# Cross attention on one core: the last transpose of a softmax put off, ring weights asked for ahead, a split sum, and a new order of the last outputs

## The chip, the core and the metric

The kernel runs on one NeuronCore of a Trainium2 chip. The time is the device time of one execution in microseconds; the figure before the change is the median of three runs. A core has five engines with a queue of instructions each: TensorE (PE, matmuls; PEld is its weight load), VectorE (DVE), ScalarE (ACT), GpSimd (POOL) and SyncE (SP), which in this kernel issues nearly all DMAs. Each queue runs in order, and engines wait for each other with semaphores. Lines such as L525 are lines of the kernel's source before the change.

## The reference, cut to what matters

`x` is 8 batches of 256 rows of 1024 values, `ctx` 8 batches of 256 rows of 1024. There are 32 heads of 32 columns. All is float32.

```
xn   = (x - mean) * rsqrt(var + 1e-5) * gamma + beta      # per row
Q    = heads(xn @ Wq.T);  K = V = heads(ctx)
p    = softmax(where(mask, Q K^T / sqrt(32), -inf))
out  = x + merge_heads(p V) @ Wout.T
```

## The kernel before, in words

**Slots.** The main loop (L870) runs over 64 slots `n`: batch `n // 8`, group of four heads `n % 8`. It is a software pipeline over groups. In slot `n` PE gets the scores of group `n + 1` (`scores`, L471), some steps of the output projection of the batch before (`product_steps`, L681), the product of the probabilities and values of group `n - 2` (`values`, L611), and a part of the queries of later batches (`make_q`, L332, or `query_product`, L432). The other engines get the softmax of group `n + 1` in the same slot. The order on each queue is the order in which the Python code emits instructions; nothing reorders it. Below, `i` is the place of a slot in its batch, `n % 8`.

**Softmax** (`softmax_parts`, L483). For each of four heads `j`, `exps(j)` masks and takes a row minimum on DVE (L506) and the exponential with its sum on ACT (L510). `normalize(j)` is a reciprocal on DVE (L517) and two scalings on POOL (L519). `blocks(j)` transposes 32 by 32 blocks on DVE into `pT` (L525), and `aside` copies half of the result on ACT into `pc` (L531), for two heads at a time. Four DMAs on SP then exchange partitions: `pT<-pT` (L591) and `pT<-pc` (L595), two of each. The last part, `tail`, holds `blocks(3)`, `aside(1)`, the four moves and, between the pairs of moves, the loads listed in `between`. `values(n)` needs it two slots later. `pT` and `pc` have three buffers each.

**A tail can be put off.** In the first batch and in softmaxes 57 to 62 it isn't emitted at once but put into `tails`, and the next softmax emits it after its own `exps(0)`. All others emit it at once (L597).

**Loads.** `between` holds, by slot, the keys (`load_k`, even slots), the values (`load_v`, odd slots), inputs of later batches, the residual rows for the outputs (`load_res`, L150, in slots `i` = 0 to 3), and `rings[n]`: weights for the queries that are kept in DRAM and brought into one SBUF tile, `ring`, three times in a batch from batch 3 on (`load_ring`, L399). T1 comes in slots `i` = 7 and 0, B11 in slot 2, T3 in slot 4, each as two transfers of 512 KB. They are used by `query_product` in slots `i` = 2, 4 and 6, and a new set can be brought in only after PE has read the old one.

**Query and output products** use a scheme of seven products of half-size blocks, with sums of blocks on POOL: `sum_x` (L422) for the inputs, `sum_at` (L664) for the attention results. A batch's seven output products accumulate in one PSUM bank; on its way DVE takes the state of the bank three times into the residual tiles (`store`, L723, and `take`, L719), and PE waits for that before it goes on in the bank. POOL has added the first product's part to three of the four residual tiles before (`add_p1`, L714). In the seventh batch's products (emitted in the last eight slots) the order differs (`ENDS`), and the sum S2 for them is emitted in slot 57.

**The end.** For the eighth batch the output projection is direct: `project` (L731) multiplies by the weights in eight chunks of 128 rows, for four outputs (`ends`: two row halves by two column halves of 512). A chunk `c` needs the attention result of head group `c`. The first output, `last`, is begun in slots 59 to 63. Then come `values(62)`, `values(63)` with their copies to SBUF (`copy_at`, L624), and the rest of the chunks, each output followed by `store`: an add on DVE and a store to DRAM. A matmul in float32 runs as two passes on PE.

Of the kernel before, what the change touches and what calls it, by code (L numbers as in the profile page):

```python
# [46 lines left out]
F32 = mybir.dt.float32  # L47
U8 = mybir.dt.uint8
AF = mybir.ActivationFunctionType
ALU = mybir.AluOpType  # L50

P = 128
# [7 lines left out]
def xattn_kernel(  # L60
# [11 lines left out]
    nc = tc.nc  # L72
    B, S, D = x.shape
# [3 lines left out]
    NQ = NC  # L77
# [9 lines left out]
    N = B * NQ  # L87
# [20 lines left out]
    NK = D // P // 2  # L108
# [14 lines left out]
    xs, ks, vs, rs = {}, {}, {}, {}  # L123
# [352 lines left out]
    def softmax(*args):  # L476
        for _ in softmax_parts(*args):
            pass
# [1 line left out]
    tails = []  # L480


    def softmax_parts(n, copies=(), between=(), hooks={}, fill=()):  # L483

        fill = list(fill)

        def fill_in():  # L490
            if fill:
                fill.pop(0)()

        pss = scs[n]
        pT = pTs[n] = ptp.tile([P, 2, NI, NH, NS, K], F32, tag="pT", name=f"pT_{n}")
        pc = asp.tile([P, NI, NH, NS, K], F32, tag="pc", name=f"pc_{n}")
        es, mns, dens = {}, {}, {}

        def exps(j, part=range(NS)):
            if 0 in part:  # L500
                es[j] = ep.tile([P, NS, T], F32, tag="e", name=f"e_{n}_{j}")
                mns[j] = sm.tile([P, NS], F32, tag="mn", name=f"mn_{n}_{j}")
                dens[j] = sm.tile([P, NS], F32, tag="den", name=f"den_{n}_{j}")
            e, mn, den = es[j], mns[j], dens[j]
            for s in part:
                nc.vector.tensor_tensor_reduce(  # L506
                    out=e[:, s, :], in0=pss[j][:, s, :], in1=mbs[n // NQ], scale=1.0,
                    scalar=NO_SCORE, op0=ALU.add, op1=ALU.min, accum_out=mn[:, s : s + 1],
                )
                nc.scalar.activation(  # L510
                    e[:, s, :], e[:, s, :], AF.Exp, bias=mn[:, s : s + 1], scale=-1.0,
                    accum_out=den[:, s : s + 1],
                )

        def normalize(j):
            rden = sm.tile([P, NS], F32, tag="rden", name=f"rden_{n}_{j}")
            nc.vector.reciprocal(rden, dens[j])  # L517
            for s in range(NS):
                nc.gpsimd.tensor_scalar(  # L519
                    es[j][:, s, :], es[j][:, s, :], rden[:, s : s + 1], 1.0,  # L520
                    ALU.mult, ALU.mult,
                )

        def blocks(j):
            nc.vector.transpose(  # L525
                pT[:, :, :, j, :, :].rearrange("p a i s k -> p (a i) s k"),
                es[j].rearrange("p s (b t) -> p b s t", t=K),
            )

        def aside(j):  # L530
            nc.scalar.copy(pc[:, :, ts(j, 2)], pT[:, 1, :, ts(j, 2)])  # L531

        if n == 0:
            for j in range(NH - 1):
                exps(j, (0,))
            yield
            exps(NH - 1, (0,))
            fill_in()
            yield
            for j in range(NH):  # L540
                exps(j, (1,))
            normalize(0)
            fill_in()
        else:
            exps(0)
            while tails:
                tails.pop()()
            late = "p1" in hooks
            if not late:
                for done in list(pvs):  # L550
                    copy_at(done)
            exps(1)
            for hook in hooks.get("soon", ()):
                hook()
            exps(2)
            normalize(0)
            for hook in hooks.get("p1", ()):
                hook()
            exps(3)
            if late:  # L560
                for done in list(pvs):
                    copy_at(done)
        if n <= NQ:
            for copy in copies:
                copy()
        for hook in hooks.get(0, ()):
            hook()
        normalize(1)
        fill_in()
        blocks(0)  # L570
        for hook in hooks.get(1, ()):
            hook()
        normalize(2)
        fill_in()
        blocks(1)
        aside(0)
        normalize(3)
        fill_in()
        blocks(2)
        while fill:  # L580
            fill_in()
        if n > NQ:
            for copy in copies:
                copy()

        def tail():
            blocks(3)
            aside(1)

            for r in range(2):  # L590
                nc.sync.dma_start(pT[ts(2 * r, K), 1], pT[ts(2 * r + 1, K), 0])  # L591
            for load in between:
                load()
            for r in range(2):
                nc.sync.dma_start(pT[ts(2 * r + 1, K), 0], pc[ts(2 * r, K)])  # L595

        if n < NQ or N - NQ < n < N - 1:  # L597
            tails.append(tail)
        else:
            tail()  # L600
        yield
# [16 lines left out]
    def copy_at(n):  # L618
        b, c = divmod(n, NQ)
        k, c = divmod(c, NK)  # L620
        if c == 0:
            ats[b, k] = atp.tile([P, NK, NS, NA, K], F32, tag="at", name=f"at_{b}_{k}")
        for r, pv in enumerate(pvs.pop(n)):
            nc.scalar.copy(  # L624
                ats[b, k][:, c, :, ts(r, 2), :], pv.rearrange("p a s k -> p s a k")
            )
# [22 lines left out]
    def operand(b, name):  # L649

        if name in ("S2", "S1"):
            return s2s[b]
        s, k = {"A11": (0, 0), "A12": (0, 1), "A21": (1, 0), "A22": (1, 1),
                "S3": (1, 0), "S4": (0, 1)}[name]
        return ats[b, k][:, :, s].rearrange("p c a k -> p c (a k)")

    def sum_at(b, name):
        if name == "S2":
            s2s[b] = up.tile([P, NK, P], F32, tag="s2", name=f"s2_{b}")
        one, two, op = {  # L660
            "S3": ("A11", "A21", ALU.subtract), "S2": ("A22", "S3", ALU.subtract),
            "S1": ("S2", "A11", ALU.add), "S4": ("A12", "S2", ALU.subtract),
        }[name]
        nc.gpsimd.tensor_tensor(operand(b, name), operand(b, one), operand(b, two), op)  # L664

    s2s, p1s = {}, {}

# [55 lines left out]
        nc.vector.tensor_tensor(r, pos[b] if po is None else po, r, ALU.add)  # L723
        nc.sync.dma_start(out[b, ts(s, P), ts(h, 512)], r)

    def project(po, b, s, h, chunks):

        for c in chunks:
            k, i = divmod(c, NK)
            w = {(0, 0): wo[:, B11], (1, 0): wo[:, B21], (1, 1): wo[:, B22], (0, 1): b12}[k, h]  # L730
            nc.tensor.matmul(  # L731
                po, ats[b, k][:, i, s].rearrange("p a k -> p (a k)"), w[:, i],
                start=(c == 0), stop=(c == NC - 1),
            )

# [94 lines left out]
    scores(0, (0,))  # L830
    for c in range(NC):
        copy_x0(1, c, nc.scalar if c < NC // 2 else nc.vector)
    first = softmax_parts(0, (partial(copy_q, 1),), (), {}, [
        partial(ln_stats, 1, 0), partial(ln_stats, 1, 1),
        partial(ln_norm, 1, 0, nc.vector), partial(ln_norm, 1, 1, nc.scalar),
    ])
# [33 lines left out]
    for n in range(N):  # L870
# [4 lines left out]
            between.append(partial(load_v, n + 1))  # L875
        elif n % 2 == 0 and n + 4 < N:
            between.append(partial(load_k, n + 4))
        between += rings[n]
        if b >= 0:
            if b == B - 2 and i - 1 in (2, 5, 6):  # L880
                between.append(partial(send, b, *ENDS_TO[i - 1]))
# [39 lines left out]
            fill = [partial(ln_stats, *args, parts=(i,)) for args in stats[n] for i in range(3)]  # L921
            fill += [partial(blocks_x, *args) for args in trans[n]]
        if n + 1 < N:
            softmax(n + 1, copies, between, hooks, fill)
        else:
            copy_at(n - 2)
            for load in between:
                load()
        if b >= 0 and i == 1:
            sum_at(b, "S2")  # L930
        if n >= NQ:
            for args in stats[n]:
                ln_stats(*args)
# [12 lines left out]
        if b >= 0:  # L946
            for name in {0: ("S3",), 2: ("S4",), 3 if b == B - 2 else 5: ("S1",)}.get(i, ()):
                sum_at(b, name)
        for slot, name in ((n + 2, "S1"), (n + 1, "S2"), (n + 1, "S4"), (n - 1, "S3")):
            if slot in firsts:  # L950
                sum_x(firsts[slot], name)
# [10 lines left out]
            nc.gpsimd.tensor_scalar(gs, gam, NEG_SCALE, 1.0, ALU.mult, ALU.mult)  # L962
        if n < NQ:
            fold(n)
        if not new_qs[n] and n - 2 > N - NQ:

            chunks = [c for c in range(NQ) if N - NQ + c <= n - 3]
            if last is None:
                last = ps_q.tile([P, 512], F32, tag="pq", name="po_last")
                made = 0  # L970
            project(last, B - 1, 0, 0, chunks[made:])
            made = len(chunks)
# [3 lines left out]
    ends = [(B - 1, s, h) for h in range(NO) for s in range(NS)]  # L976
    pos = {end: ps_s.tile([P, 512], F32, tag="sc", name=f"po_{end[1]}_{end[2]}") for end in ends[1:]}
    pos[ends[0]] = last
    values(N - 2)
    copy_at(N - 2)  # L980
    again = xp.tile([P, NS, D], F32, tag="x", name="x_again")
    for s in range(NS):
        nc.sync.dma_start(again[:, s, :], x[B - 1, ts(s, P), :])
    for b, s, h in ends:
        rs[b, s, h] = again[:, s, ts(h, 512)]
    project(last, *ends[0], range(made, NQ - 2))
    project(pos[ends[1]], *ends[1], range(NQ - 2))
    values(N - 1)
    copy_at(N - 1)
    project(pos[ends[2]], *ends[2], range(NQ - 1))  # L990
    for i, end in enumerate(ends):
        project(pos[end], *end, range((NQ - 2, NQ - 2, NQ - 1, 0)[i], NQ))
        store(*end, pos[end])


# [38 lines left out]
```

## Time and profile before

| what | us |
|---|---|
| runs | 585.6, 586.97, 590.12 (median 586.97) |
| the profiled execution, its own time | 585.12 |
| its span, first to last instruction | 583.3 |
| PE busy | 570.0 (98%) |
| PE weight loads busy | 392.6 (67%) |
| DVE busy | 453.4 (78%) |
| ACT busy | 412.2 (71%) |
| POOL busy | 393.0 (67%) |
| DMA | 119.02 MB, 204 GB/s on average |

The granted PE clock is full throughout. The time between two starts of the scores is a slot's length: some 6 to 10 us. Ends of matmuls are modelled in the profile, so that a busy PE can hide short waits. A number in brackets after an instruction is the idle time of its engine just before it, and what ended that.

### The profile page before, as it was taken

To read this page: it belongs to the slowest core of one execution; us is meant where nothing else is said; L and a number is where in the kernel's file an instruction comes from. 1 tells how busy PE (TensorE), PEld (TensorE's weight loads), DVE (VectorE), ACT (ScalarE), POOL (GpSimd) and SP (SyncE) were. 2 spreads that over 40 slices of the span, in tenths; PEclk is the share of its full clock that TensorE was granted. 3 is DMA by queue.
4 is the path that set the end of the run, shared out by engine and by line. 5 is a ranking of instruction groups with operands and counts; after the bars stand their busy time and mean duration, and the time that the engine had idled before them with its cause. 6 is when DMAs were issued, how large, how long until landed. Compare 5 with 4: busy or idle time off the path is not lost.

```text
span 583.3 us, 19985 instructions
## 1 busy us (share of the span) xinstructions
PE 570.0 (98%) x7160; PEld 392.6 (67%) x7160; DVE 453.4 (78%) x1685; ACT 412.2 (71%) x1425; POOL 393.0 (67%) x662
## 2 busy tenths in 40 slices
PE   8999999999999999999999999999999999999997
PEld 7787785766657767667766776676776776645443
DVE  5878887888778888788886898688976787689701
ACT  4788887777668867687775976769775876679800
POOL 1568898899789886677448765587636864559700
PEclk9999999999999999999999999999999999999999
DMA  8557789756786778766887668857757776448551
GB/s 310 218 159 223 219 242 234 218 180 166 221 261 202 213 223 240 221 191 164 255 233 213 187 188 247 239 172 228 207 157 237 223 193 186 127 135 238 159 160 72
DMA packets 47907, 119.02 MB, mean 204 GB/s; under 512 B 9152, under 2 KB 9664, under 8 KB 47808
## 3 DMA queue, kind: packets, MB, share of 16 engines
q1 hardware_dynamic: 47520, 117.74, 68.6%
q8 instruction: 57, 0.93, 0.7%
q14 instruction: 42, 0.34, 0.2%
q10 hardware_dynamic: 288, 0.01, 0.0%
HBM read 66.33 MB, written 11.53 MB: 133 GB/s over the span
## 4 chain that ended last, share of the span: by engine, by line
PE 60%; POOL 14%; DVE 10%; DMA 7%; issue 4%; ACT 2%; SPq 2%; POOLq 0%; DVEq 0%; ACTq 0%
PE po_S L681 14%; PE pq_A L432 10%; POOL e L519 10%; PE pq L332 8%; PE sc L471 7%; PE pv L611 7%; PE po_A L681 6%; DVE e L506 4%; PE po L731 4%; DVE pT L525 3%; PE pq_S L432 2%; DMA wq<-in_wq_dram 2%; POOL sx L422 2%; DMA x<-in_x_dram 1%; DMA pT<-pT 1%
## 5 line engine op out<-in xcount | busy, mean ns | idle before, releaser
L519 POOL TENSOR_SCALAR e<-e,rden 128x256 f32<-128x256 f32 x512 | 235.7, 478 | 95.6 <-DVE rden L517 93.2
L510 ACT ACTIVATE e<-e,mn 128x256 f32<-128x256 f32 x512 | 253.9, 500 | 38.6 <-DVE mn L506 38.5
L525 DVE STREAM_TRANSPOSE pT<-e 128x512 f32<-128x512 f32 x256 | 181.2, 708 | 63.5 <-POOL e L519 52.5
L506 DVE CUSTOM_DVE_ANT_0 e<-sc,mb 128x256 f32<-128x256 f32 x512 | 185.5, 415 | 19.4 <-PE sc L471 19.1
L531 ACT COPY pc<-pT 128x512 f32<-128x512 f32 x128 | 79.0, 617 | 85.8 <-DVE pT L525 43.3
L510 ACT ACTIVATION_READ_ACCUMULATOR e<-e,mn 128x1 f32 x512 | 97.7, 191 | 0.0
L332 PE MATMUL pq<-xnT,wq 128*128 128x256 f32 (+1 forms) x368 | 84.1, 382 | 1.3 <-ACT qa L339 1.2
L332 PEld LDWEIGHTS pq<-xnT,wq 128*128 128x128 f32 x368 | 68.7, 190 | 15.8 <-issue 3.8
L611 PE MATMUL pv<-pT,v 64*32 64x128 f32 x4096 | 74.7, 274 | 1.9 <-ACT at L624 1.0
L611 PEld LDWEIGHTS pv<-pT,v 64*32 64x32 f32 x4096 | 57.3, 105 | 27.3 <-issue 12.8
L471 PEld LDWEIGHTS sc<-k,qa 32*128 32x128 f32 x1024 | 46.7, 184 | 42.9 <-issue 23.7
L681 PE MATMUL po_S<-wo,at 128*128 128x512 f32 x152 | 74.6, 608 | 0.9 <-DVE r L719 0.9
L471 PE MATMUL sc<-k,qa 32*128 32x256 f32 x1024 | 74.6, 401 | 0.1
L681 PE MATMUL po_A<-wo,at 128*128 128x512 f32 x128 | 60.6, 608 | 0.4 <-ACT qa L341 0.4
L681 PE MATMUL po_S<-wo,s 128*128 128x512 f32 x104 | 50.2, 607 | 0.5 <-DVE r L723 0.5
L517 DVE RECIPROCAL rden<-den 128x2 f32<-128x2 f32 x256 | 37.7, 147 | 7.5 <-ACT e L510 6.1
L506 DVE DVE_READ_ACCUMULATOR2_ANT mn<- 128x1 f32 x512 | 42.5, 83 | 0.0
L432 PEld LDWEIGHTS pq_A<-xnT,wq 128*128 128x128 f32 x320 | 37.3, 192 | 4.8 <-issue 3.8
L681 PEld LDWEIGHTS po_S<-wo,at 128*128 128x128 f32 x152 | 25.8, 190 | 21.2 <-issue 19.3
L681 PEld LDWEIGHTS po_A<-wo,at 128*128 128x128 f32 x128 | 22.6, 189 | 25.4 <-issue 21.4
L432 PE MATMUL pq_A<-xnT,wq 128*128 128x128 f32 x320 | 37.3, 275 | 0.0
L714 POOL TENSOR_TENSOR r<-r,p 128x512 f32<-128x512 f32 x18 | 23.1, 1284 | 14.1 <-DMA r<-in_x_dram 14.1
(82 smaller groups left out, 591.6 us busy)
## 6 DMA issues: line engine op xcount, KB each, us to landing
v<-in_kv_dram SPq DMA_DIRECT2D x32, 512.0 KB, 4.1
pT<-pT SPq DMA_DIRECT2D x128, 128.0 KB, 2.5
pT<-pc SPq DMA_DIRECT2D x128, 128.0 KB, 5.1
ring<-kept_T SPq DMA_DIRECT2D x18, 512.0 KB, 6.0
k<-in_kv_dram SPq DMA_DIRECT2D x32, 256.0 KB, 3.0
x<-in_x_dram SPq DMA_DIRECT2D x14, 512.0 KB, 5.1
r<-in_x_dram SPq DMA_DIRECT2D x28, 256.0 KB, 4.4
out_dram<-r SPq DMA_DIRECT2D x28, 256.0 KB, 3.8
```

The lines of the kernel that those rows point to most:

```text
L332: nc.tensor.matmul(pqs[n], wq[:, o, c, :], xnTs[b](c), start=(c == 0), stop=(c == NC - 1),)
L432: nc.tensor.matmul(pqs[b][:, o, :], w[:, c], x_[:, c], start=begins and o + c == 0, stop=c == NK - 1, skip_group_check=True,)
L471: nc.tensor.matmul(scs[n][j][:, s, :], qa[r, n % NQ, ts(s, P)], ks[n - n % 2][r, n % 2, :], start=True, stop=True,)
L506: nc.vector.tensor_tensor_reduce(out=e[:, s, :], in0=pss[j][:, s, :], in1=mbs[n // NQ], scale=1.0, scalar=NO_SCORE, op0=ALU.add, op1=ALU.m ...
L510: nc.scalar.activation(e[:, s, :], e[:, s, :], AF.Exp, bias=mn[:, s : s + 1], scale=-1.0, accum_out=den[:, s : s + 1],)
L517: nc.vector.reciprocal(rden, dens[j])
L519: nc.gpsimd.tensor_scalar(es[j][:, s, :], es[j][:, s, :], rden[:, s : s + 1], 1.0, ALU.mult, ALU.mult,)
L525: nc.vector.transpose(pT[:, :, :, j, :, :].rearrange("p a i s k -> p (a i) s k"), es[j].rearrange("p s (b t) -> p b s t", t=K),)
L531: nc.scalar.copy(pc[:, :, ts(j, 2)], pT[:, 1, :, ts(j, 2)])
L611: nc.tensor.matmul(pvs[n][r][j * HD : (j + 1) * HD], vs[n - n % 2][ts(r, 2 * K), i, ds(n % 2 * P + j * HD, HD)], pT[ts(r, 2 * K), :, i, j, ...
L681: nc.tensor.matmul(po, operand(b, name)[:, c], wo[:, which, c], start=begins and c == 0, stop=c == NK - 1, skip_group_check=not begins,)
L731: nc.tensor.matmul(po, ats[b, k][:, i, s].rearrange("p a k -> p (a k)"), w[:, i], start=(c == 0), stop=(c == NC - 1),)
```

## The change

There are five edits.

1. `DEFERRED = range(1, 5)`: the tails of softmaxes with `n % 8` from 1 to 4 are put off, in all batches.
2. `rings[n]` leaves `between` and becomes `ahead`, emitted just before the place where the tail is either emitted or put off.
3. S2 of the seventh batch is emitted in two parts: chunks 0 to 2 at the end of slot 56, after S3, and chunk 3 in slot 57.
4. The chunks of the last projections are put in another order around `values(62)` and `values(63)`. The first output is begun in slots 59 to 62 and no longer in slot 63.
5. The last of the four outputs is made in two column parts, 384 and 128 wide, each with its own matmuls, add and store; the second uses a PSUM tile of the `ps_v` pool.

```diff
+    DEFERRED = range(1, 5)
+
+    def softmax_parts(n, copies=(), ahead=(), between=(), hooks={}, fill=()):
...
-        if n < NQ or N - NQ < n < N - 1:
+        for load in ahead:
+            load()
+        if n < NQ or n % NQ in DEFERRED or N - NQ < n < N - 1:
             tails.append(tail)
         else:
             tail()
...
-    def sum_at(b, name):
-        if name == "S2":
+    def sum_at(b, name, c=slice(0, NK)):
+        if name == "S2" and c.start == 0:
...
-        nc.gpsimd.tensor_tensor(operand(b, name), operand(b, one), operand(b, two), op)
+        nc.gpsimd.tensor_tensor(
+            operand(b, name)[:, c], operand(b, one)[:, c], operand(b, two)[:, c], op
+        )
...
-    def project(po, b, s, h, chunks):
+    def project(po, b, s, h, chunks, cols=slice(0, 512)):
...
-                po, ats[b, k][:, i, s].rearrange("p a k -> p (a k)"), w[:, i],
+                po, ats[b, k][:, i, s].rearrange("p a k -> p (a k)"), w[:, i, cols],
...
-        between += rings[n]
...
-            softmax(n + 1, copies, between, hooks, fill)
+            softmax(n + 1, copies, rings[n], between, hooks, fill)
...
-            sum_at(b, "S2")
+            sum_at(b, "S2", *((slice(NK - 1, NK),) if b == B - 2 else ()))
...
+            if i == 0 and b == B - 2:
+                sum_at(b, "S2", slice(0, NK - 1))
...
-        if not new_qs[n] and n - 2 > N - NQ:
+        if not new_qs[n] and N - NQ + 2 < n < N - 1:
...
-    values(N - 2)
-    copy_at(N - 2)
...
-    project(last, *ends[0], range(made, NQ - 2))
-    project(pos[ends[1]], *ends[1], range(NQ - 2))
+    project(pos[ends[1]], *ends[1], range(NK))
+    project(last, *ends[0], range(made, NQ - 3))
+    values(N - 2)
+    copy_at(N - 2)
+    project(pos[ends[1]], *ends[1], range(NK, NQ - 3))
+    project(pos[ends[2]], *ends[2], range(NK))
+    project(last, *ends[0], (NQ - 3,))
+    project(pos[ends[1]], *ends[1], (NQ - 3,))
     values(N - 1)
     copy_at(N - 1)
-    project(pos[ends[2]], *ends[2], range(NQ - 1))
-    for i, end in enumerate(ends):
-        project(pos[end], *end, range((NQ - 2, NQ - 2, NQ - 1, 0)[i], NQ))
+    project(pos[ends[2]], *ends[2], range(NK, NQ - 1))
+    for i, end in enumerate(ends[:3]):
+        project(pos[end], *end, range((NQ - 2, NQ - 2, NQ - 1)[i], NQ))
         store(*end, pos[end])
+
+    b, s, h = ends[3]
+    r = rs.pop(ends[3])
+    for cols in (slice(0, 384), slice(384, 512)):
+        po = pos[ends[3]] if cols.start == 0 else ps_v.tile([P, P], F32, tag="pv", name="po_end")
+        po = po[:, : cols.stop - cols.start]
+        project(po, *ends[3], range(NQ), cols)
+        nc.vector.tensor_tensor(r[:, cols], po, r[:, cols], ALU.add)
+        nc.sync.dma_start(out[b, ts(s, P), ds(512 * h + cols.start, cols.stop - cols.start)], r[:, cols])
```

More of the change, by code (lines that the diff above doesn't have):

```diff
@@ L480, in xattn_kernel @@
     tails = []
-    def softmax_parts(n, copies=(), between=(), hooks={}, fill=()):
+    DEFERRED = range(1, 5)
+    def softmax_parts(n, copies=(), ahead=(), between=(), hooks={}, fill=()):
         fill = list(fill)
@@ L832, in xattn_kernel @@
         copy_x0(1, c, nc.scalar if c < NC // 2 else nc.vector)
-    first = softmax_parts(0, (partial(copy_q, 1),), (), {}, [
+    first = softmax_parts(0, (partial(copy_q, 1),), (), (), {}, [
         partial(ln_stats, 1, 0), partial(ln_stats, 1, 1),
```

## The prediction

> **What bounds the kernel now.** I first cut the span into stages and read how long TensorE (PE) is busy in each. The columns are the stage, its length, then busy time and instruction count of PE, of PE's weight loads, DVE, ACT and POOL, the clock and the DMAs.
>
> ```profile
> 0.00:24.74 24.74, 20.76 (x144) 17.55 (x145) 17.38 (x54) 12.15 (x34) 7.53 (x21) 1.00 0.81 300
> 24.74:93.53 68.79, 67.35 (x817) 53.93 (x817) 58.27 (x226) 57.59 (x196) 55.99 (x90) 1.00 0.72 203
> 93.53:240.00 146.47, 146.47 (x1826) 98.57 (x1829) 119.16 (x445) 106.86 (x369) 123.02 (x190) 1.00 0.75 217
> 240.00:447.00 207.00, 204.98 (x2759) 144.11 (x2760) 170.35 (x630) 153.94 (x537) 132.13 (x234) 1.00 0.72 209
> 447.00:510.00 63.00, 63.00 (x836) 45.22 (x835) 49.00 (x183) 43.84 (x157) 41.10 (x73) 1.00 0.64 183
> 510.00:543.60 33.60, 32.63 (x449) 16.66 (x447) 29.02 (x120) 28.94 (x103) 24.68 (x44) 1.00 0.65 189
> 543.60:583.30 39.70, 34.85 (x339) 16.60 (x338) 10.25 (x32) 8.91 (x30) 8.58 (x14) 1.00 0.39 120
> ```
>
> From 93.5 to 240 us and from 447 to 510 PE has no gap. The edit removes no matmul and no PE work, so it can win only where PE waits: 2.0 us in the middle, 1.0 before 543.6, 4.85 at the end, and a little at the start. Second, PE's own timeline: what ends each gap (in brackets).
>
> ```profile
> 93.53 3.70 PE L681 MATMUL po_A<-wo,at 128*128 128x512 f32 x8 [0.41 <-ACT qa L341]
> 265.87 1.12 PE L681 MATMUL po_S<-wo,at 128*128 128x512 f32 x2 [0.40 <-DVE r L719]
> 277.89 2.02 PE L432 MATMUL pq_A<-sx,ring 128*128 128x128 f32 x16 [0.22 <-DMA ring<-kept_T]
> 280.36 2.05 PE L432 MATMUL pq_A<-sx,ring 128*128 128x128 f32 x16 [0.45 <-DMA ring<-kept_T]
> 316.70 1.96 PE L681 MATMUL po_S<-wo,s 128*128 128x512 f32 x4 [0.20 <-DVE r L723]
> 326.55 1.98 PE L681 MATMUL po_S<-wo,at 128*128 128x512 f32 x4 [0.24 <-DVE r L719]
> 385.82 1.96 PE L681 MATMUL po_S<-wo,s 128*128 128x512 f32 x4 [0.26 <-DVE r L723]
> 395.67 1.98 PE L681 MATMUL po_S<-wo,at 128*128 128x512 f32 x4 [0.25 <-DVE r L719]
> 519.97 3.70 PE L681 MATMUL po_A<-wo,s 128*128 128x512 f32 x8 [0.97 <-POOL s L664]
> 553.52 1.31 PE L611 MATMUL pv<-pT,v 64*32 64x128 f32 x64 [1.04 <-ACT at L624]
> ```
>
> These are all the gaps from 93 us on that are 0.2 us or longer. Ends of matmuls are modelled, so I size gaps by slot length, from one start of the scores (L471) to the next, against the same slot of another batch. Slot 28: 257.75 to 266.92 is 9.17, slot 36 takes 8.51: 0.66 lost. Slot 30: 9.49 against 8.51, 0.98. Slots 34 and 42: 8.94 and 9.00 against 8.51, 0.43 and 0.49. Slots 35 and 43: 9.88 against 9.37, 0.51 each. Together 3.6 us. Third, I followed one gap (slot 28) back through the queues:
>
> ```profile
> 254.85 0.87 SPq L399 DMA_DIRECT2D ring<-kept_B  x2
> 255.77 0.42 SPq L150 DMA_DIRECT2D r<-in_x_dram  x1
> 263.81 1.28 POOL L714 TENSOR_TENSOR r<-r,p 128x512 f32<-128x512 f32 x1 [3.62 <-DMA r<-in_x_dram]
> 265.12 0.69 DVE L719 TENSOR_TENSOR r<-po_S,r 128x512 f32<-128x512 f32 x1 [1.59 <-POOL r L714]
> ```
>
> A 256 KB residual, asked for just behind 1 MB of ring weights, lands 8.0 us after its issue; POOL waits 3.6 us for it, DVE's `take` for POOL, PE for DVE. Last, the end: PE stops at about 579.5, then
>
> ```profile
> 579.52 0.69 DVE L723 TENSOR_TENSOR x_again<-po,x_again 128x512 f32<-128x512 f32 x1 [6.17 <-PE po L731]
> 580.24 0.33 SPq L724 DMA_DIRECT2D out_dram<-x_again  x1
> ```
>
> and 3.06 us from that issue to the end of the span.
>
> [...] The trace shows 0.20 to 0.33 us of idle weight loads at each change between scores, values and full-size matmuls; the edit must not add such changes. [...] SP does show idle stretches ahead of L591 waiting for ACT. [...] quiet 256 KB stores here landed in 2.4 us[...].
>
> **The change, part by part.**
>
> *Tail put off (softmax 9 to 12 of each eight, slots with n mod 8 = 0 to 3, batches 1 to 6 of the loop).* No instruction is added. The transpose of head 3 on DVE (0.71 us), its ACT copy (0.62) and SP's four moves go behind the next softmax's first scores. DVE no longer sits at L525 for POOL (0.2 to 0.27 us in most slots, 52.5 us of waits by the group's row), since the next exponentials fill in; ACT's L531 (43.3 us of waits on pT) likewise. Applied to slot 35: ACT runs its layer-norm pass (1.24) at 322.1 rather than 322.74 because L531 is behind it, so the exponentials that DVE's reciprocal waits for (0.77 at 324.99) end about 0.4 earlier; `take` at 325.81 becomes about 325.4 and the gap (0.51) goes nearly whole: 0.4, and 0.4 in slot 43. Slots 34 and 42: `store` at L723 only gains the 0.20 that DVE idled before the transpose, as its work ahead is the same: 0.2 each. There POOL's late start is set by the sum L422, which waits for the moves of x (4.6 us idle at 307.34); that stays. Slot 9: L341, the copy of a second query chunk, sat behind L531 (waiting until 92.48); free of it, it ends near 92.5 and PE wants it at 93.1: 0.45.
> Everything else in the tail is put off too: the k, v and residual loads. Keys and values have more than a slot of slack. Residual (0,1): in slot 34 issue moves from 315.47 to about 317.6 (scores' exponentials 1.4, transpose 0.6, copy 0.6, two moves 1.2, v load 0.6 after 313.6), landing in 4.1 us at 321.7; POOL wants it at 322.87. Cover 1.2 us. The moves themselves: in slot 36 the last was issued at 335.07; some 3 us later plus 5 us to land makes 343, values need it at 346.6. Cover 3.5 us.
>
> *Ring weights ahead.* No instruction added; SP issues both halves as soon as PE has read the old ones. B11: at about 247.4 (behind the store at 246.87) instead of 254.85, so the 1 MB is gone when residual (1,1) is asked for at about 256; it lands near 260, POOL arrives at 260.2, `take` no longer waits 1.59: slot 28 gets back its 0.66. T3: in slot 28 SP had issued the old moves by 266.6 and stood idle till 270.29; with the put-off tail taking it to about 270, the ring goes at 270 instead of 272.79, 2.8 us earlier than landings at 277.75 and 280.32: slot 30 gets back 0.98. The cost, a wait on PE in front of the new tail's moves, is nothing while PE is done (265.5) before SP comes (270); if not, the moves use up some of their 3.5 us.
>
> Middle together: 0.4+0.4+0.2+0.2+0.45+0.66+0.98 = 3.3 us (0 to 4.0).
>
> *S2 of batch 7 in two parts.* POOL's 1.26 us sum at 518.65 is what PE waited for. Three chunks go a slot earlier, right after S3 (ends 508.8), into 6.2 us of POOL idle before 514.98: free. The last chunk, 128 columns: at least a quarter, 0.32; at most 0.55 (the longest tiny POOL row, L231); I take 0.35. Ready at 519.0 instead of 519.91: 0.9 (0.7 to 0.97).
>
> *Order of the last projections.* Values 62 waited 1.04 for `copy_at(61)`. Now five chunks (0.86 each, two passes of 0.43) stand before it, so it starts near 555.7, after that copy (553.6). Values 63 start near 562.8, its moves were issued by 557.4: no wait. Number of chunks (28) and of mode changes is unchanged. Gain 1.04.
>
> *Last output by columns.* PE: 16 passes of 0.43 = 6.86 become 16 at three quarters (0.32) plus 16 of 128 columns (0.112, the spacing of L432's): 6.94, a loss of 0.08. The closing add shrinks from 0.69 to about 0.28 (from DVE rows of 256 and 512 columns: 0.42 and 0.69): 0.4. The closing store is 64 KB rather than 256[...]. One DVE op, one DMA more, both beside PE. Gain 0.75 (0.3 to 1.0).
>
> Sum 3.3+0.9+1.0+0.75 = 5.95. The profiled execution took 585.12 (span 583.3): 579.2. It is below all three times shown (585.6, 586.97, 590.12); from the median the sum gives 581.0. Waits on DMA landings vary between runs and the edit widens their margins, so I go between: **580.5**.
>
> **Rivals.**
> (1) *The middle barely moves.* PE's waits there come from POOL and DVE work, not from order: the sum L422 still waits for moves, residuals come later. For: `store` in slots 34 and 42 has the same work ahead. Against: slots 28 and 30 are DMA orders that plainly change. Only 0.9+1.0+0.75 and a little remain: 587-3 = 584 (582.5 to 585). Chance 0.25.
> (2) *Residuals become the bound: slower.* Decides when residual (0,1) lands after 322.87, that is takes over 5.3 us from issue, with POOL's L714 and DVE's `take` behind it. Residuals behind big loads took up to 8.0 us; here a v load of 512 KB is just ahead. At 8.0 POOL, `take` and PE are 2.7 us late in slot 35 and its like: six batches, 16 us, less 6: 596. Against: residuals behind a v load landed in 4.1 (315.47 to 319.57). Chance 0.05.
> (3) *Put-off moves reach values too late*: needs over 3.5 us more; past it 24 slots pay. At 0.3 us each 7 us eaten: 588. Chance 0.05.
> (4) *More than forecast*: gaps of other runs, larger than the profiled one's, go as well: 577.5. Chance 0.1.
> Forecast 0.55 (578.5 to 582.5).
>
> **How the numbers follow.** About 1% (5.9 us) is what a measurement can tell here; below 581.1 is faster. Two thirds of the forecast case and all of (4): 0.37+0.1, with the best of (1) 0.49. Slower is (2): 0.05. Range 577 to 585 leaves out (2), (3) and the edges of (1) and (4).
>
> **What would show it.** Right: slots 28 and 30 at 8.5 us, no PE gap on ring or L719, ring B11 issued just behind the slot-26 store, L664's 128-column sum at about 0.35, no gap before values 62, and under 3.2 us from the last matmul to the end. Wrong: POOL idle at L714 growing, gaps before values on pT moves, or slots 34, 35 still over 8.5 and 9.4.

## The result, and the profile after

| | us |
|---|---|
| before, median of 17 runs | 587.52 (585.17 to 590.12) |
| changed, median of 17 runs | 590.92 (585.95 to 597.3) |
| ratio, 95% interval | 1.0051, 1.003 to 1.0072 |
| profiled execution before, its span | 585.12, 583.3 |
| profiled execution changed, its span | 589.45, 587.7 |

The change makes the kernel half a per cent slower. The forecast was 580.5 with a range of 577 to 585: the prediction is wrong by 10 us and on the wrong side. Numbers of lines are from here on those of the changed kernel, unless a line is said to be of before: the softmax's transposes L528, its scalings L522, ACT's copy L534, the moves L594 and L598, output steps L688, `add_p1` L721, `take` L726, `store` L730 and its DMA L731, `project` L738, S2 L669, values L616.

First the same view by stages (columns as in the prediction; the cuts are the starts of the same slots).

```profile
93.50:239.50 146.00, 145.99 (x1823) 98.26 (x1821) 116.47 (x438) 106.62 (x370) 118.94 (x182) 1.00 0.72 209
239.50:453.23 213.73, 206.99 (x2762) 144.83 (x2761) 171.24 (x632) 153.33 (x537) 133.80 (x236) 0.99 0.72 203
453.23:516.00 62.77, 61.89 (x833) 44.97 (x833) 48.44 (x183) 43.64 (x157) 43.80 (x76) 1.00 0.70 195
516.00:549.91 33.91, 32.98 (x451) 16.79 (x449) 28.96 (x120) 28.94 (x103) 24.18 (x45) 1.00 0.66 188
549.91:587.70 37.79, 34.71 (x355) 18.48 (x354) 10.39 (x33) 8.91 (x30) 8.55 (x14) 1.00 0.43 126
```

The end, the last of these stages, is as forecast: 37.8 us, 39.7 before. The stage from 240 us on, where 2.0 us were to be won, is 213.7 us long, 207.0 before, and PE has 6.7 us of gaps in it. Next PE's timeline, the same kind of rows as in the prediction: all that have a gap over 0.5 us after 93 us and before the end.

```profile
248.80 1.96 PE L688 MATMUL po_S<-wo,s 128*128 128x512 f32 x4 [2.44 <-DVE r L730]
318.68 1.95 PE L688 MATMUL po_S<-wo,s 128*128 128x512 f32 x4 [1.52 <-DVE r L730]
390.09 3.21 PE L688 MATMUL po_S<-wo,s 128*128 128x512 f32 x4 [2.67 <-DVE r L730]
460.97 1.95 PE L688 MATMUL po_S<-wo,s 128*128 128x512 f32 x4 [0.88 <-POOL sx L422]
532.12 3.70 PE L688 MATMUL po_A<-wo,at 128*128 128x512 f32 x8 [0.93 <-ACT ends L706]
```

The gaps that the prediction listed on `ring` and on `take` are gone. Those ahead of `po_S<-wo,s`, 0.20 and 0.26 before, are now 1.52 and 2.67, and there are two more. The first four rows are in the slots 26, 34, 42 and 50, the fifth is in slot 59. By slot length, from score start to score start:

| slot | before | changed | gain | forecast |
|---|---|---|---|---|
| 26 | 8.51 | 11.19 | -2.68 | none |
| 34 | 8.94 | 10.27 | -1.33 | 0.2 |
| 42 | 9.00 | 13.04 | -4.04 | 0.2 |
| 50 | 8.51 | 9.62 | -1.11 | none |
| 28, 30 | 9.17, 9.49 | 8.51, 8.51 | 1.64 | 1.64 |
| 35, 43 | 9.88, 9.88 | 9.37, 9.75 | 0.64 | 0.8 |
| 9 | 9.04 | 8.56 | 0.48 | 0.45 |
| 21 | 8.51 | 8.79 | -0.28 | none |
| 58 and 59 | 13.64 | 13.48 | 0.16 | 0.9 |
| last stretch | 39.71 | 37.75 | 1.96 | 1.8 |

With 0.2 us from the start and small differences in other slots this is -4.3 us, the difference of the two spans. The rows that gain come to 4.9 us, near the forecast's 5.95; four slots that the sum gave 0.4 us take 9.2 us away.

Each column is one execution, and the same slots of the same loop can differ from one execution to the next. The profile of edits 4 and 5 alone (below), whose loop up to slot 58 is that of the kernel before, has slot 28 at 8.51, slot 30 at 8.50, slot 9 at 9.98 and slot 42 at 9.89. A row that moves by less than 1 us shows nothing by itself; it has to come back in other profiles.

**Where it is lost.** I followed slot 26 back as the prediction had followed slot 28: PE waits for `store` on DVE, which has the softmax's transposes before it, which wait for POOL's scalings, which stand behind the sum L422. POOL's and DVE's timelines after:

```profile
239.73 1.26 POOL L422 TENSOR_TENSOR sx<-xnT 128x512 f32<-128x512 f32 x1 [7.02 <-issue]
381.02 1.27 POOL L422 TENSOR_TENSOR sx<-xnT 128x512 f32<-128x512 f32 x1 [7.76 <-DMA xnT<-xe]
241.94 0.71 DVE L528 STREAM_TRANSPOSE pT<-e 128x512 f32<-128x512 f32 x1 [6.26 <-POOL e L522]
247.97 0.69 DVE L730 TENSOR_TENSOR r<-po_A,r 128x512 f32<-128x512 f32 x1
```

The first row names no releaser (`issue`); the view of the line of the moves of `x`, L319, puts these 7.0 us to them. In the kernel before, POOL's idle ahead of the same sum was half as long:

```profile
236.48 1.26 POOL L422 TENSOR_TENSOR sx<-xnT 128x512 f32<-128x512 f32 x1 [3.52 <-PE po_A L681]
```

The sum needs the moves of `x`, `xnT<-xe`, which SP issues as the last of the slot's moves. SP's timeline for slot 23 shows what stands before them; first before (old numbers: moves L591 and L595), then after:

```profile
225.45 1.81 SPq L591 DMA_DIRECT2D pT<-pT  x2
227.31 0.65 SPq L144 DMA_DIRECT2D v<-in_kv_dram  x1
228.00 0.45 SPq L399 DMA_DIRECT2D ring<-kept_T  x1
228.66 1.15 SPq L595 DMA_DIRECT2D pT<-pc  x2
229.86 2.50 SPq L319 DMA_DIRECT2D xnT<-xe  x4
```

```profile
225.82 0.52 SPq L399 DMA_DIRECT2D ring<-kept_T  x1
226.45 1.63 SPq L594 DMA_DIRECT2D pT<-pT  x2
228.13 0.57 SPq L144 DMA_DIRECT2D v<-in_kv_dram  x1
232.56 1.14 SPq L598 DMA_DIRECT2D pT<-pc  x2
233.75 2.49 SPq L319 DMA_DIRECT2D xnT<-xe  x4
```

The columns are start and length of the issues. After, SP stands still from 228.70 to 232.56: `pT<-pc` overwrites what `pT<-pT` reads, so SP waits until that has landed, and `pT<-pT` now goes behind the ring's 512 KB. Before, the ring was issued between the two pairs, where SP had to pass the time anyway. The moves of `x` are not concerned with `pT` at all, but they stand behind that wait in SP's queue: they go out 3.9 us later, at 233.75 instead of 229.86. SP's waits for this landing over the whole run, in total, times and longest, before and after, and one of POOL's after:

```profile
SPq L595 <- DMA pT<-pT: 24.2, 27, 2.8
```

```profile
SPq L598 <- DMA pT<-pT: 81.6, 36, 5.4
POOL sx L422 <- DMA xnT<-xe: 21.5, 3, 7.8
```

The rise from 24.2 to 81.6 us is not the loss. SP is held behind the other rings too: behind T3, which is emitted in slot 28, from 272.19 to 276.09, 3.9 us as well. There no moves of `x` come next in the queue, and slots 28 to 31 take 8.51 each. With T1's first half back (the first experiment) SP still waits 69.8 us for this landing, and the loss is gone. The hold costs where POOL needs what stands behind it: it waits for moves of `x` 28.5 us in four sums, the 7.0 us above among them, and 4.7 us in two sums before.

The row of 24.2 us stood in the trace of before; the prediction makes no use of it.

### The profile page after: what moved, and what is told of

Read it like the earlier page. It is cut to its first block, busy times and chain, and to the rows that moved or that the text cites. A ratio compares the mean times of both kernels' runs of the same rounds, so it can differ in the third digit from the quotient of the medians.

```text
span 587.7 us, 20003 instructions
## 1 busy us (share of the span) xinstructions
PE 571.3 (97%) x7176; PEld 395.6 (67%) x7176; DVE 451.3 (77%) x1686; ACT 410.6 (70%) x1425; POOL 393.4 (67%) x663
## 4 chain that ended last, share of the span: by engine, by line
PE 70%; DMA 8%; DVE 7%; POOL 7%; issue 6%; ACT 1%; SPq 1%; POOLq 0%; DVEq 0%; ACTq 0%
PE po_S L688 17%; PE pq_A L432 11%; PE pq L332 11%; PE sc L471 9%; PE pv L616 8%; PE po_A L688 5%; POOL e L522 4%; PE pq_S L432 4%; PE po L738 3%; DVE e L509 3%; DMA pT<-pT 3%; DVE pT L528 2%; DMA wq<-in_wq_dram 2%; DMA x<-in_x_dram 1%; PE po_last L738 1%
## 5 line engine op out<-in xcount | busy, mean ns | idle before, releaser
L522 POOL TENSOR_SCALAR e<-e,rden 128x256 f32<-128x256 f32 x512 | 235.6, 478 | 92.2 <-DVE rden L520 89.0
L528 DVE STREAM_TRANSPOSE pT<-e 128x512 f32<-128x512 f32 x256 | 181.0, 707 | 71.3 <-POOL e L522 60.2
L534 ACT COPY pc<-pT 128x512 f32<-128x512 f32 x128 | 78.6, 614 | 76.9 <-DVE rden L520 51.6
L616 PE MATMUL pv<-pT,v 64*32 64x128 f32 x4096 | 74.3, 274 | 1.1 <-ACT qa L339 1.1
L616 PEld LDWEIGHTS pv<-pT,v 64*32 64x32 f32 x4096 | 57.2, 105 | 26.1 <-issue 11.9
L688 PE MATMUL po_S<-wo,at 128*128 128x512 f32 x152 | 74.3, 606 | 0.0
L688 PE MATMUL po_A<-wo,at 128*128 128x512 f32 x128 | 60.6, 609 | 0.9 <-ACT ends L706 0.9
L688 PE MATMUL po_S<-wo,s 128*128 128x512 f32 x104 | 51.6, 622 | 7.5 <-DVE r L730 6.6
L688 PEld LDWEIGHTS po_A<-wo,at 128*128 128x128 f32 x128 | 22.6, 190 | 25.9 <-issue 21.5
L688 PEld LDWEIGHTS po_S<-wo,at 128*128 128x128 f32 x152 | 25.8, 190 | 19.7 <-issue 19.3
L721 POOL TENSOR_TENSOR r<-r,p 128x512 f32<-128x512 f32 x18 | 23.0, 1280 | 18.1 <-DMA r<-in_x_dram 18.0
```

What stands on the lines that cost most here:

```text
L522: nc.gpsimd.tensor_scalar(es[j][:, s, :], es[j][:, s, :], rden[:, s : s + 1], 1.0, ALU.mult, ALU.mult,)
L528: nc.vector.transpose(pT[:, :, :, j, :, :].rearrange("p a i s k -> p (a i) s k"), es[j].rearrange("p s (b t) -> p b s t", t=K),)
L616: nc.tensor.matmul(pvs[n][r][j * HD : (j + 1) * HD], vs[n - n % 2][ts(r, 2 * K), i, ds(n % 2 * P + j * HD, HD)], pT[ts(r, 2 * K), :, i, j, ...
L688: nc.tensor.matmul(po, operand(b, name)[:, c], wo[:, which, c], start=begins and c == 0, stop=c == NK - 1, skip_group_check=not begins,)
```

## The experiments

Theory A: edit 2 loses the time in slots `i` = 7, where the ring's T1 (first half, 512 KB) goes ahead of the tail and holds SP on `pT<-pT`, with the moves of `x` behind. The rivals were that the put-off tails (edit 1) lose it, and that the ring takes bandwidth from the moves of `x` rather than holding their issue. All ratios are against runs of the kernel before that were taken along with each experiment; their medians are 588.11, 587.6 and 587.3.

**T1's first half back between the moves; the other rings stay ahead.** Against the changed kernel:

```diff
             between.append(partial(load_k, n + 4))
+        if n % NQ == NQ - 1:
+            between += rings[n]
+            rings[n] = []
```

> The changed kernel with one thing undone: the first half of the T1 ring weights (slots 23, 31, 39, 47) is asked for between the pairs of moves again, as before the change; B11, T3 and the second half of T1 stay ahead. Theory A (queue): those 512 KB, just ahead of the moves pT<-pT, make them land late; pT<-pc waits for that on SP, and the moves of x behind it come 3 to 4 us late, so POOL's sum L422, the scalings, DVE's store and PE in slots 26, 34, 42 and 50 do. Then these slots go from 11.2, 10.3, 13.0 and 9.6 us to 8.5 to 9.0, and the median is near 582 (580.5 to 584). Theory B (put-off transpose): the transposes between the exponentials of slots i = 1 and 2 make the store late. Then nothing changes: 590 to 591.

Measured 581.25 (580.53 to 582.79), ratio 0.9895 (0.9872 to 0.9918). Slots 26, 34, 42 and 50 take 8.78, 9.52, 8.56 and 8.51 us; slot 34 misses the expected 8.5 to 9.0. One load of 512 KB in each of four batches, moved by three issues in SP's queue, is 9.7 us by the medians (9.2 by the two ratios).

**Edit 2 alone**, the kernel before with `rings[n]` handed over as `ahead`:

```diff
-        between += rings[n]
...
-            softmax(n + 1, copies, between, hooks, fill)
+            softmax(n + 1, copies, rings[n], between, hooks, fill)
```

> The kernel before with the ring weights ahead alone, no tail put off. Theory A: slots 26, 34, 42 and 50 lose about what the changed kernel lost there (9 us in all), slots 28 and 30 gain 1.6: near 595 (591 to 598). Theory B: no loss there, only the gain: near 586.

Measured 591.98 (588.98 to 597.83), ratio 1.0064 (1.0034 to 1.0093), from which the longest run is left out. The loss is there without any new put-off tail. The profile is of that longest run, so it is read for places only: slots 28 and 30 are at 8.51 and slots 26, 34 and 42 at over 12.

**Edit 1 alone**, the kernel before with the wider condition:

```diff
-        if n < NQ or N - NQ < n < N - 1:
+        if n < NQ or n % NQ in range(1, 5) or N - NQ < n < N - 1:
```

> The kernel before with the tails put off alone, ring weights where they were. Theory A: slot 9 gains 0.5, slots 35 and 43 0.4 to 0.5 each, slots 26, 34, 42 and 50 stay within 0.3 of before; 586 (585 to 587). Theory B: the loss of some 9 us is here: 594 to 596.

Measured 590.64 (587.95 to 595.14), ratio 1.0061 (1.004 to 1.0082). The expectation is missed: edit 1 alone loses as well, but elsewhere. Slots 26 and 42 take 8.51 and 9.24; slots 28, 36 and 44 take 10.13, 10.41 and 11.01, where 9.17, 8.51 and 8.51 stood, and slot 21 takes 10.21 instead of 8.51 (not followed further). Its timeline in slot 28, SP, POOL, DVE and PE:

```profile
256.79 0.86 SPq L399 DMA_DIRECT2D ring<-kept_B  x2
257.70 0.42 SPq L150 DMA_DIRECT2D r<-in_x_dram  x1
265.63 1.27 POOL L714 TENSOR_TENSOR r<-r,p 128x512 f32<-128x512 f32 x1 [4.67 <-DMA r<-in_x_dram]
266.93 0.69 DVE L719 TENSOR_TENSOR r<-po_S,r 128x512 f32<-128x512 f32 x1 [3.17 <-POOL r L714]
267.68 1.12 PE L681 MATMUL po_S<-wo,at 128*128 128x512 f32 x2 [0.90 <-DVE r L719]
```

The residual behind the 1 MB of B11 was late before by 1.59 us at `take`; put off with the tail, it is asked for 1.93 us later (257.70 instead of 255.77) and `take` waits 3.17. This is the mechanism of the prediction's rival 2, with another residual: the ring in front of it is what makes it decide. In the changed kernel edit 2 takes B11 out of the way.

**T1 and B11 both back**, as the first experiment with `if n % NQ in (2, NQ - 1)`:

> The kernel with T1's first half back between the moves, and B11 (slots i = 2) back between them as well, so that residual (1,1) again stands right behind 1 MB in a tail that is put off. If that is what made the put-off tails alone slower, slots 28, 36 and 44 go from 8.5 to 10.1, 10.4 and 11.0 us as there: 581.25 + 6 = 587 (585 to 589). If not, 581 to 582.

Measured 589.8 (585.2 to 592.18), ratio 1.0023 (1.0002 to 1.0044): 8.5 us more by the medians than with T1 alone back, 7.5 by the two ratios, and above the expected 585 to 589. Slots 28, 36 and 44 take 10.22, 10.18 and 10.33, as expected; slots 21, 26 and 42 are longer too (10.09, 9.35 and 10.46), which isn't explained. POOL's wait:

```profile
POOL r L721 <- DMA r<-in_x_dram: 27.1, 9, 4.8
```

In the changed kernel that wait is 18.0 us. So edit 2 is two edits with opposite signs. For B11, in slots `i` = 2, it is what keeps edit 1 from costing time; for T1, in slots `i` = 7, it is the loss.

**The moves of `x` first.** The ring stays ahead of the tail in slots `i` = 7, but the moves of `x` go between the ring and the tail:

```diff
-            softmax(n + 1, copies, rings[n], between, hooks, fill)
+            ahead = list(rings[n])
+            if n % NQ == NQ - 1:
+                ahead += [partial(move_x, *args) for args in moves[n]]
+                moves[n] = []
+            softmax(n + 1, copies, ahead, between, hooks, fill)
```

> The changed kernel with only this moved: in slots i = 7 the last four moves of x stand right behind the ring transfer and ahead of the tail's moves. The ring stays ahead of everything. Theory A1 (held on the queue): the moves of x were late because SP waits for pT<-pT to land before it issues pT<-pc, and they stand behind that. Then they are out some 6 us earlier, L422 waits less than before the change, slots 26, 34, 42 and 50 take 8.5 to 8.8 us: 580 (578.5 to 582). Theory A2 (shared bandwidth): the 512 KB in the DMA queues slow the moves of x themselves. Then these slots stay at 9.5 to 12 us and the time at 587 to 591.

Measured 580.48 (579.17 to 581.97), ratio 0.9876 (0.9837 to 0.9915). Its SP and POOL timelines in slot 23:

```profile
229.22 0.38 SPq L399 DMA_DIRECT2D ring<-kept_T  x1
229.65 2.50 SPq L319 DMA_DIRECT2D xnT<-xe  x4
232.26 1.16 SPq L594 DMA_DIRECT2D pT<-pT  x2
233.46 0.59 SPq L144 DMA_DIRECT2D v<-in_kv_dram  x1
237.36 1.14 SPq L598 DMA_DIRECT2D pT<-pc  x2
237.16 1.27 POOL L422 TENSOR_TENSOR sx<-xnT 128x512 f32<-128x512 f32 x1 [2.10 <-DMA v<-in_kv_dram]
```

The ring is directly ahead of the moves of `x`, and SP still stands still for 3.3 us before `pT<-pc` (3.9 in the changed kernel). But the sum on POOL idles 2.1 us instead of 7.0, and slots 26, 34, 42 and 50 take 8.97, 8.51, 8.51 and 8.51. It is the moves' place behind the hold on SP's queue that costs, not the ring's bytes as such.

**The dose.** Both halves of T1 (1 MB) go ahead in slots `i` = 7:

```diff
-        for slots, name in (((n - 3, n - 2), "T1"), ((n, n), "B11"), ((n + 2, n + 2), "T3")):
+        for slots, name in (((n - 3, n - 3), "T1"), ((n, n), "B11"), ((n + 2, n + 2), "T3")):
```

> The changed kernel with the dose doubled: both halves of T1 (1 MB) ahead in slots i = 7, none in slots i = 0. A1: pT<-pT lands another 1.2 to 2 us later, and with it each of slots 26, 34, 42 and 50: 5 to 8 us more than the changed kernel, 597 (594 to 600). If the place of the first half does not matter, no change: 590.

Measured 595.89 (594.16 to 599.98), ratio 1.0147 (1.01 to 1.0194). SP and POOL in slot 23:

```profile
228.33 0.88 SPq L399 DMA_DIRECT2D ring<-kept_T  x2
229.31 1.15 SPq L594 DMA_DIRECT2D pT<-pT  x2
230.51 0.57 SPq L144 DMA_DIRECT2D v<-in_kv_dram  x1
236.06 1.15 SPq L598 DMA_DIRECT2D pT<-pc  x2
242.02 1.26 POOL L422 TENSOR_TENSOR sx<-xnT 128x512 f32<-128x512 f32 x1 [9.07 <-PE pv L616]
```

SP's hold (end of the `v` issue to the start of `pT<-pc`) is 4.98 us, against 3.86 with 512 KB ahead; POOL's idle is 9.07 against 7.02. POOL's row names a step of PE as what ended its idle; that the sum waits for the moves of `x` here too is inferred from the order on SP. A megabyte ahead doesn't double the hold: the second 512 KB adds 1.1 us.

**The other parts.** Edits 4 and 5 alone, on the kernel before (the diff of the front, from the second half of `project` on):

```diff
+    def project(po, b, s, h, chunks, cols=slice(0, 512)):
...
+        if not new_qs[n] and N - NQ + 2 < n < N - 1:
...
+    project(pos[ends[1]], *ends[1], range(NK))
+    project(last, *ends[0], range(made, NQ - 3))
+    values(N - 2)
+    copy_at(N - 2)
...
+    for cols in (slice(0, 384), slice(384, 512)):
```

> The kernel before with the new order of the last projections and the last output by columns alone. Both theories: the stretch from the scores of group 63 to the end takes 37.75 us rather than 39.71, as in the changed kernel, nothing else moves: 2.0 us less, near 585.5.

Measured 585.29 (584.44 to 585.99), ratio 0.9959 (0.9942 to 0.9977), 2.8 us by the medians and 2.4 by the ratio. The last stretch is 37.72 us, 39.71 before. But the two spans differ by only 0.7 us, and the expectation that nothing else moves is missed: slots 8, 9, 27, 42 and 46 are 0.5 to 0.9 us longer than in the profile of before, slots 28 and 30 take 8.51 and 8.50 instead of 9.17 and 9.49, in a loop that is the same. The residual of slot 28, still behind the 1 MB of B11, landed 6.4 us after its issue, not 8.0, and the wait on PE was gone:

```profile
257.33 0.42 SPq L150 DMA_DIRECT2D r<-in_x_dram  x1
263.74 1.28 POOL L714 TENSOR_TENSOR r<-r,p 128x512 f32<-128x512 f32 x1 [1.75 <-DMA r<-in_x_dram]
```

Edit 1 taken out, T1 back as in the first experiment (only the first of these two edits is shown):

```diff
-        if n < NQ or n % NQ in DEFERRED or N - NQ < n < N - 1:
+        if n < NQ or N - NQ < n < N - 1:
```

> The kernel with T1's first half back between the moves (581.25), and no tails put off beyond those of before: what edit 1 is worth once the rings are right. If by its own terms: slot 9 loses 0.5 and slots 35 and 43 0.5 each again, slots 28 and 30 stay at 8.5: 582.7 (582 to 584). If putting off is what makes the order safe for residuals, more: 585. If it costs, below 581.

Measured 583.54 (580.94 to 586.26), ratio 0.9927 (0.9905 to 0.9949). With T1 back, edit 1 is worth 2.3 us by the medians, 1.9 by the two ratios and 3.2 by the two profiles. Slots 9, 27, 35 and 43 are each 0.5 longer without it, and slot 42 takes 9.80 instead of 8.56; slot 21 is 0.5 shorter without it.

S2 whole again, T1 back (again only what is new):

```diff
-            sum_at(b, "S2", *((slice(NK - 1, NK),) if b == B - 2 else ()))
+            sum_at(b, "S2")
...
-            if i == 0 and b == B - 2:
-                sum_at(b, "S2", slice(0, NK - 1))
```

> The kernel with T1's first half back between the moves, and S2 of batch 7 whole again. If slot 59's wait on the copy L706 takes back what slot 58 gained: slot 58 at 6.9 and slot 59 at 6.65, in all 0.1 us more than 581.25, not to be told from it. If the split is worth what was forecast: 0.9 more, 582.1.

Measured 581.49 (579.89 to 584.38), ratio 0.9901 (0.9868 to 0.9935), no different from the 0.9895 with the split. Slots 58 and 59 take 6.93 and 6.65, with the split 5.86 and 7.62: together 13.58 and 13.48. What PE gains in slot 58 it waits for in slot 59.

**A version that beats both.** In slots `i` = 7 the moves of `x` go first, then the tail, then the ring; and in slot 58 the steps on PE and the copy of an output part on ACT that PE waits for in slot 59 (L706) are emitted ahead of the softmax's `aside(0)`:

```diff
-            ((1, keep_p1), (2, take_po_q), *((i, copy_po, i) for i in range(3, 8))) if ends else
+            ((1, keep_p1), (2, take_po_q), *((i, copy_po, i) for i in range(4, 8))) if ends else
...
-            softmax(n + 1, copies, rings[n], between, hooks, fill)
+            ahead, behind_tail = list(rings[n]), []
+            if n % NQ == NQ - 1:
+                behind_tail, ahead = ahead, [partial(move_x, *args) for args in moves[n]]
+                moves[n] = []
+            if b == B - 2 and i == 2:
+                project_steps(n, 2)
+                hooks.setdefault(1, []).append(partial(copy_po, b, 3))
+            softmax(n + 1, copies, ahead, between, hooks, fill)
+            for load in behind_tail:
+                load()
...
-        project_steps(n, 2)
+        if not (b == B - 2 and i == 2):
+            project_steps(n, 2)
```

> A version drawn from the findings: the changed kernel with, in slots i = 7, the moves of x first, then the tail, then the first half of T1; and in slot 58 the copy of the bank that PE waits for in slot 59 (L706) ahead of the copy L534. A1: slots 26, 34, 42 and 50 at 8.5 us, slot 59 at 6.7 rather than 7.6: 579 (577.5 to 581). A2 gives the same for the first part. If L706 was not what slot 59 waits for, slot 59 stays at 7.6.

Measured 579.91 (579.28 to 580.86), ratio 0.9868 (0.9836 to 0.99). SP and POOL in slot 23:

```profile
227.29 2.60 SPq L319 DMA_DIRECT2D xnT<-xe  x4
229.99 1.16 SPq L594 DMA_DIRECT2D pT<-pT  x2
231.19 0.58 SPq L144 DMA_DIRECT2D v<-in_kv_dram  x1
232.32 1.14 SPq L598 DMA_DIRECT2D pT<-pc  x2
233.52 0.58 SPq L399 DMA_DIRECT2D ring<-kept_T  x1
233.34 1.28 POOL L422 TENSOR_TENSOR sx<-xnT 128x512 f32<-128x512 f32 x1
```

SP's hold is 0.55 us, and POOL goes into the sum without idling. Slots 34 and 42, 8.94 and 9.00 before, take 8.51, as they do in the moves-first kernel: what the prediction had seen there, 0.43 and 0.49, and given up to "waits for the moves of x", is to be had by the moves' place. Slot 59 takes 6.85 instead of 7.62, but slot 60 has 7.10 instead of 6.65, so about 0.3 of that edit remains. Its ratio and that of the moves-first kernel have overlapping intervals; which is faster isn't settled.

## Why the prediction was wrong, step by step

**The step that failed** is *Ring weights ahead*, and in it the sentence on cost: "No instruction added", and the cost, "a wait on PE in front of the new tail's moves, is nothing while PE is done (265.5) before SP comes (270)". It asked only whether SP would have to wait to issue the ring. It didn't ask what 512 KB issued ahead of `pT<-pT` do to that transfer's landing, who waits for it (SP, in front of `pT<-pc`), and what else is queued behind on SP (the moves of `x`). It worked out the gain for B11 and T3 and never worked the third ring, T1, at all, which is in slots with their own moves. In place of nothing the profile shows SP held for 3.9 us in slot 23, the moves of `x` out 3.9 us later, 7.0 us of idle time on POOL ahead of their sum, and 9.2 us of longer slots in four batches; 9.7 us lie between the medians with T1 ahead and with T1 back.

**Linked to it,** *slots 34 and 42*: "There POOL's late start is set by the sum L422, which waits for the moves of x (4.6 us idle at 307.34); that stays." The chain was seen and named, and then taken to be untouched by an edit that changes what SP does just ahead of those moves. Forecast 0.2 each, measured -1.33 and -4.04; and with the moves first, 0.43 and 0.49 against the profile of before.

**Right, with their sizes:** slot 9, 0.45 against 0.48 (8.57 in all profiles with the tails put off but one, which has 9.84); slot 35, 0.4 against 0.51 (slot 43 0.13 in the changed kernel, where it follows the disturbed slot 42, and 0.51 with T1 back). Slot 35 takes 9.36 to 9.48 in every profile with the tails put off and 9.66 to 9.89 in every one without. The order of the last projections and the last output by columns, 1.79 together, gave 1.96, and nearly the same when edited in alone. In the view of DVE after, the closing add was forecast at 0.28:

```profile
582.87 0.56 DVE L1013 TENSOR_TENSOR x_again<-po,x_again 128x384 f32<-128x384 f32 x1 [4.47 <-PE po L738]
584.66 0.29 DVE L1013 TENSOR_TENSOR x_again<-po_end,x_again 128x128 f32<-128x128 f32 x1 [1.23 <-PE po_end L738]
```

The closing store of 64 KB landed 1.7 us after its issue, and from that issue to the end of the span it is 2.7 us, 3.06 before: 0.3 us less. What the forecast of 0.75 for the last output counted on the smaller store was the author's estimate; no trace of before showed it.

**The size came out, but the cause isn't shown:** slots 28 and 30, 0.66 and 0.98. They take 8.51 in the changed kernel and 8.50 to 8.57 in all profiles with B11 and T3 ahead, but 8.51 and 8.50 also with edits 4 and 5 alone, where both rings are still between the moves. The gain was sized from one execution in which the residual and the ring happened to be late. An estimate for many runs: the kernel with T1 back and no new tails put off (0.9927) against edits 4 and 5 alone (0.9959) gives 1.9 us for B11, T3 and T1's second half ahead and the split S2 together, near the 1.64, but the two intervals overlap.

**S2, 0.9 forecast, about 0.1 measured.** POOL's part is a little dearer than thought and went as described:

```profile
515.30 0.99 POOL L669 TENSOR_TENSOR s<-at,at 128x384 f32<-128x384 f32 x1
525.10 0.45 POOL L669 TENSOR_TENSOR s<-at,at 128x128 f32<-128x128 f32 x1
```

(0.45 where I took 0.35 from the bounds 0.32 and 0.55.) But the prediction didn't say what is late next: PE, a slot later, 0.93 us on ACT's copy L706.

**Rivals.** Rival 1, the middle barely moves, is not what happened: it moves in both directions. Rival 2, slower through a residual, had the right shape, a put-off or moved DMA that lands behind a big load and holds POOL, DVE and PE, and named the wrong transfer; it does happen with edit 1 alone and with B11 back. It got 0.05, since I had checked one residual's landing and no move's. A sign that the prediction had named, POOL idle ahead of `add_p1` growing, did come in the changed kernel (18.0 us in 13 waits, 14.1 in 7 before), but PE has no gap on `take` from it. Rival 3, moves too late for the values, didn't show: no gap on `pT` at L616. With T1 back the spans differ by 4.5 us where 5.95 was forecast, and 0.8 of what is missing is S2. The median, 581.25, lies in the range, and that is partly luck: against the kernel before it is 6.9 us less by the medians, since the profile from which the sum was worked out (585.12) was quicker than the median of before.

**Two loose readings.** The parts listed for the issue of residual (0,1) add up to 318.0, not 317.6, so its cover was 0.8 us rather than 1.2. And the 0.20 to 0.33 us of idle weight loads aren't peculiar to the changes between scores, values and full-size matmuls: in the profile of before (257 to 285 us) weight loads also idle 0.24 us between two full-size ones, and 0.76 us ahead of the scores. No run here shows what such a change costs, and the forecast doesn't rest on it.

## What to carry to other kernels

Before moving a DMA ahead in a queue, ask three things of every transfer behind it: when does it land now, who waits for that landing, and what is queued behind the waiter. SP's queue has to be followed like an engine's: here SP stood still 3.9 us for the landing of `pT<-pT` in slot 23, and the moves of `x` behind that went out 3.9 us later. With these moves ahead of the wait POOL idled 2.1 us before their sum and not 7.0, and with the ring's 512 KB put back into the wait the time was 9.7 us less by the medians. And an edit that is applied by one line to several loads is several edits; here they had opposite signs. With the tails put off, T1 ahead lost 9.2 to 9.7 us and B11 ahead saved 7.5 to 8.5. Last, a gain that is sized from a wait in one profiled execution needs a second execution of the same code: two of the waits that this change set out to remove were absent from another profile of the same loop.

## What the runs showed of the hardware

In some of the profiles PE's granted clock falls after a gap on PE. In the changed kernel this happens once between the start and the end: the gap of 2.67 us at 390 us is followed by four matmuls that take 3.21 us, where the same four take 1.95 and 1.96 elsewhere. The windows there, with length, busy times, and as third number from the end the clock:

```profile
386.00:390.00 4.00, 1.42 (x13) 1.23 (x12) 3.93 (x15) 2.20 (x8) 3.64 (x4) 1.00 0.36 89
390.00:394.00 4.00, 3.91 (x12) 1.60 (x16) 3.38 (x15) 3.26 (x14) 3.77 (x9) 0.58 0.75 215
```

From 391 to 394 us the clock is 0.50, from 394 to 395 it is 0.97. So a part of slot 42's 4.04 is not the wait but what follows it: 1.26 us in these four matmuls. Another 0.38 us falls into slot 43, whose scores take 1.53 us instead of 1.15. With both halves of T1 ahead the mean clock over the profiled run is 0.989 (0.997 in the changed kernel, 1.00 with T1 back). The gaps ahead of `po_S<-wo,s` in the slots 26, 34 and 42 of both kernels, with the time of the four matmuls behind each:

| kernel | slot | gap on PE | the four matmuls |
|---|---|---|---|
| changed | 26 | 2.44 | 1.96 |
| changed | 34 | 1.52 | 1.95 |
| changed | 42 | 2.67 | 3.21 |
| both halves of T1 ahead | 26 | 3.90 | 3.01 |
| both halves of T1 ahead | 34 | 2.17 | 3.48 |
| both halves of T1 ahead | 42 | 2.86 | 3.75 |

The length of the gap alone doesn't sort them: 1.96 us behind a gap of 2.44 and 3.48 behind one of 2.17. What decides it isn't shown here.

By the mean clocks of its 17 runs (what each is short of 1, times the span) the changed kernel loses, as an estimate, 2.5 us to the lower clock on average; with T1 back all runs have 0.999 or 1.000. So about a quarter of the 9.7 us is this. But the clock is not the main reason for the wide spread of the changed kernel's times (11.4 us from lowest to highest, 5.0 before): its runs have mean clocks of 0.991 to 1.000, but the quickest (585.95) and the slowest (597.3) both have 0.997. What makes the spread stays open, and so does why slot 50 loses only 1.1 us with the same order on SP and a sum that POOL waits for as long (7.5 us).
